# The 17-tap convolution of a graph network: one 136-point transform per graph in place of two 80-point windows

## The chip, the core and the metric

The kernel runs on one NeuronCore of a Trainium2 chip. The metric is device time in microseconds (us) of one execution. The kernel before has a median of 1908.61 us over 3 runs (1906.02 to 1911.41).

## The reference

A batch of 128 graphs with 128 nodes and 256 channels, all in float32, passes through two layers. The change concerns one convolution of the first layer, `conv2_w` with 17 taps along the node axis:

```python
h = relu(layernorm(x))                                  # (128, 128, 256)
xc = transpose(h, (0, 2, 1))
c = relu(bn1(conv1d(xc, conv1_w, pad=0)))               # 1 tap, 256 -> 256 channels
c = bn2(conv1d(c, conv2_w, pad=8))                      # 17 taps, 256 -> 256 channels
x_conv = transpose(relu(c + xc), (0, 2, 1))
s = h @ w_se.T + b_se;  A = exp(-dist(s, s)) * adj;  msg = relu(h @ w_msg.T + b_msg)
x_nmp = A @ msg
gi = concat([x_conv, x_nmp]) @ w_ih.T + b_ih;  gh = h @ w_hh.T + b_hh
r, z = sigmoid(gi_r + gh_r), sigmoid(gi_z + gh_z);  n = tanh(gi_n + r * gh_n)
x = x + (1 - z) * n + z * h
# second layer: five small graph convolutions on the first 25 nodes of each graph, added to x
```

## The kernel before, in words

The 17-tap convolution is done in the frequency domain. Each graph's 128 nodes are cut into two windows of 64 outputs; each window is transformed with `LW = 80` points (64 outputs and 16 neighbours), so there are `NP_ = 40` pairs of rows per window (real and imaginary part of a frequency). The work goes through these stages:

1. **Heads with the spectra of the weights** (`heads`, `some_spectra`). The graphs go in blocks of four (`BB = 4`). For each block: load x (`ln`, L184), layer norm on VectorE (L193 to L204), transpose on TensorE (L214), the 1-tap convolution (L228), a bias on VectorE (L231) and a ReLU on ScalarE (L232), then the forward transform (L243, `fd`, 160 columns: two windows of 80) and its copy into the big tile X in SBUF (L249 VectorE, L251 ScalarE). Between the blocks the taps are transformed: `weight_spectra` multiplies 17-row slices of the taps, four of them at partitions 0, 32, 64 and 96, with the 80 columns of `gt` (L167), and copies the results out of four PSUM banks (L173, L175). The spectra go to DRAM (`vd`, L177). Each step is 16 products; 32 steps are spread over the first 16 blocks.
2. **Frequencies of the first half** (`spectral`). X holds 64 graphs times two windows, 128 rows, so the whole batch needs two halves. For every frequency p the spectra of the weights are read from DRAM (`v`, L296, through SP's queue), GpSimd adds two of them (`vs`, L311), and six products of 128 rows by 256 columns follow (L314 two, L319 four; four products at p = 0, L304). VectorE adds (L320) into `ys`, which ScalarE's queue writes to DRAM (`yd`).
3. **Heads of the second half**, 16 blocks, with no taps left. Their first loads are issued in the course of stage 2 (`heads_begin`, called from `amid` at p = 16 and later); the weights of the gates are loaded here.
4. **Frequencies of the second half**, with GpSimd's sums for the gate weights (`gate_weights`) in between.
5. **Gates**, 32 blocks, some three quarters of the span: message passing (L535, L573, L585, L600), the inverse transform (`conv_out`), and the recurrent gates as Strassen-like products (L649), the second layer (L914, L974, L893) interleaved.

`conv_out` rebuilds the convolution of a block from `ym` (rows 0 to 127 of the 160 rows of each graph) and `yr` (the other 32 rows of each of the four graphs, together 128 rows). For each half o of the channels it takes one PSUM bank, four products with `idm` (L512, 128 columns each) and one with `idr` (L515, all 128 rows, 256 columns), then VectorE scales and adds (L517) and ScalarE applies the ReLU (L518). It is a generator: half 1 runs some steps after half 0, from `beside_gates`, which deals these pieces out between the products of the gates.

All PSUM tiles come from one pool of eight banks (`bank()`), handed out in a ring in the order in which the program asks: the ninth request gets the bank of the first, and its first product waits until that bank has been read out. TensorE takes its instructions in order.

SP's queue issues nearly all loads in an order written out by hand up to the end of stage 3 (`manual_schedule`); GpSimd's order is by hand up to the end of stage 4; the rest is placed by the scheduler.

Of the kernel before, what the change touches and what calls it, by code (L numbers as in the profile page):

```python
# [13 lines left out]
P = 128  # L14
# [4 lines left out]
HG = 64  # L19
OUTW = 64  # L20
LW = 80
NP_ = LW // 2
WCH = 64
NR = 2 * LW - P
# [51 lines left out]
def gnn_kernel(ctx: ExitStack, tc: tile.TileContext, io, out0: bass.AP, out1: bass.AP):  # L76
# [6 lines left out]

    NBH = HG // BB
    NH = B // HG

# [16 lines left out]
    fd = hc.tile([P, 2 * LW], F32)  # L103
# [46 lines left out]
    yd = [dram.tile([HG, 2, LW, D], F32, tag=f"yd{h}", name=f"yd{h}") for h in range(NH)]  # L150
# [9 lines left out]
    def weight_spectra(pool, c, q, w2):  # L160

        sp = pool.tile([P, LW, WCH], F32, tag="sp", name="sp", bufs=2)
        for t in range(WCH // 16):
            ps = [bank() for _ in range(4)]
            for j in range(4):
                for r in range(4):
                    nc.tensor.matmul(ps[r][:, j * LW:(j + 1) * LW], w2[32 * r:32 * r + KW, 4 * t + j, :],  # L167
                                     gt[32 * r:32 * r + KW, :], start=True, stop=True)
            for r in range(4):
                o0 = t * 16 + 4 * r  # L170
                dst, s = sp[:, :, o0:o0 + 4], ps[r][:, :4 * LW].rearrange("p (j d) -> p d j", j=4)
                if r == 3 and t < WCH // 16 - 1:
                    nc.vector.tensor_copy(dst, s)  # L173
                else:
                    nc.scalar.copy(dst, s)  # L175
            yield
        nc.scalar.dma_start(vd[c, q], sp)  # L177
# [57 lines left out]
    def head_spectra(X, i):  # L235
        h1 = h1s.pop(i)
        g0 = (i * BB) % HG
        for c in range(C):
            xv = X[:, c].rearrange("p a k (w g) -> p (a k) w g", w=2)
            for h in range(BB // 2):  # L240
                ps = bank()
                for bb in range(2):
                    nc.tensor.matmul(ps[:, bb * 2 * LW:(bb + 1) * 2 * LW], h1[:, 2 * h + bb, c * P:(c + 1) * P], fd,  # L243
                                     start=True, stop=True)
                s = ps[:, :4 * LW].rearrange("p (g w d) -> p d w g", g=2, w=2)
                dst = xv[:, :, :, g0 + 2 * h:g0 + 2 * h + 2]
                for w in range(2):
                    if h:
                        nc.vector.tensor_copy(dst[:, :, w], s[:, :, w])  # L249
                    else:  # L250
                        nc.scalar.copy(dst[:, :, w], s[:, :, w])  # L251

    def heads_begin(wk, xk, ahead, h):

        i = h * NBH
        for k in range(ahead):
            head_load(xk, ahead, i + k, nc.sync)
        yield
        for k in range(3):
            head_stats(wk, i + k)  # L260
            yield
            if k < 2:
                head_norm(i + k)
        head_turn(wk, i)

    def heads(wk, xk, ahead, X, h, between):

        i0, i1 = h * NBH, (h + 1) * NBH
        for i in range(i0, i1 + 1):
            if i + ahead < i1:  # L270
                head_load(xk, ahead, i + ahead, nc.sync)
            if i < i1:
                head_conv1(wk, i)
            between()
            if i + 1 < i1:
                head_turn(wk, i + 1)
            if i + 2 < i1:
                head_norm(i + 2)
            between()
            if i > i0:  # L280
                head_spectra(X, i - 1)
            if h == 0 and i % 2:
                between()
            if i + 3 < i1:
                head_stats(wk, i + 3, h1s[i] if h else None)

    def spectral(bp, X, h, amid):

        for p0 in range(0, NP_, 4):
            amid.get(p0, lambda: None)()  # L290
            ys = bp.tile([P, 4, 2, D], F32, tag="ys", name="ys", bufs=2)
            for p in range(p0, p0 + 4):
                if p % 2 == 0:
                    v = bp.tile([P, C, D // WCH, 4, WCH], F32, tag="v", name="v", bufs=3)
                    for c in range(C):
                        nc.sync.dma_start(v[:, c], vd[c, :, :, 2 * p:2 * p + 4, :].rearrange("q i d o -> i q d o"))  # L296
                vr, vi = v[:, :, :, 2 * (p % 2), :], v[:, :, :, 2 * (p % 2) + 1, :]
                a, d = X[:, :, p, 0, :], X[:, :, p, 1, :]
                y = ys[:, p - p0]
                ps = bank()  # L300
                if p == 0:
                    for k, (u, w) in enumerate(((a, vr), (d, vi))):
                        for c in range(C):
                            nc.tensor.matmul(ps[:, k * D:(k + 1) * D], u[:, c], w[:, c], start=c == 0, stop=c == C - 1)  # L304
                    nc.scalar.copy(y.rearrange("p k o -> p (k o)"), ps)
                    continue

                s = bp.tile([P, C, P], F32, tag="s", name="s", bufs=2)
                nc.vector.scalar_tensor_tensor(s, a, -2.0, d, op0=ALU.mult, op1=ALU.subtract)  # L309
                vs = bp.tile([P, C, D // WCH, WCH], F32, tag="vs", name="vs", bufs=3)  # L310
                nc.gpsimd.tensor_tensor(vs, vr, vi, op=ALU.add)  # L311
                p1 = bank()
                for c in range(C):
                    nc.tensor.matmul(p1[:, :D], a[:, c], vs[:, c], start=c == 0, stop=c == C - 1)  # L314
                k1 = bp.tile([P, D], F32, tag="k1", name="k1", bufs=2)
                nc.scalar.copy(k1, p1[:, :D])  # L316
                for k, (u, w) in enumerate(((s, vi), (d, vr))):
                    for c in range(C):
                        nc.tensor.matmul(ps[:, k * D:(k + 1) * D], u[:, c], w[:, c], start=c == 0, stop=c == C - 1)  # L319
                nc.vector.tensor_tensor(y, ps.rearrange("p (k o) -> p k o", k=2),  # L320
                                        k1[:, None, :].to_broadcast([P, 2, D]), op=ALU.add)
            for w in range(2):
                nc.scalar.dma_start(yd[h][:, w, 2 * p0:2 * p0 + 8, :].rearrange("g d o -> g (d o)"),
                                    ys[w * HG:(w + 1) * HG].rearrange("p a k o -> p (a k o)"))

# [27 lines left out]

    with front as es:
        hk = es.enter_context(tc.tile_pool(name="hk", bufs=1))
        xp = es.enter_context(tc.tile_pool(name="xp", bufs=1))
        X = xp.tile([P, C, NP_, 2, P], F32)
        order = es.enter_context(ExitStack())
        order.enter_context(tc.manual_schedule(engines={nc.gpsimd.engine}))
        sync_order = order.enter_context(ExitStack())  # L360
        sync_order.enter_context(tc.manual_schedule(engines={nc.sync.engine}))
        with ExitStack() as ws:
# [5 lines left out]
            ahead = 5  # L368
# [38 lines left out]
            heads(hk, xk, ahead, X, 0, some_spectra)  # L407
            while spectra or todo:
                some_spectra()
        gw = ctx.enter_context(tc.tile_pool(name="gw", bufs=1, side="right", reuse_waits="tile"))  # L410
        xk = es.enter_context(tc.tile_pool(name="xk1", bufs=1, reuse_waits="tile"))
        bp = es.enter_context(tc.tile_pool(name="bp", bufs=1, reuse_waits="tile"))
# [8 lines left out]
        def small_loads():  # L421
# [3 lines left out]

        begin = heads_begin(hk, xk, 3, 1)
        sums = gate_weights()
        amid = {p: lambda: next(begin, None) for p in range(16, NP_, 4) if p != 20}
        spectral(bp, X, 0, amid)
        for _ in begin:  # L430
            pass

        def gate_loads():
            yield
            small_loads()
            yield
# [3 lines left out]
            yield  # L440
            nc.sync.dma_start(wih[:, C:], io["wih"][D:].rearrange("(c p) o -> p c o", p=P))
            yield
            yield
            nc.sync.dma_start(whh, io["whh"].rearrange("(c p) o -> p c o", p=P))

        loads = gate_loads()
        heads(hk, xk, 3, X, 1, lambda: next(loads, None))
        sync_order.close()
        spectral(bp, X, 1, {p: lambda: next(sums, None) for p in range(4, NP_, 4)})
# [8 lines left out]
    loaded, hts = {}, {}  # L458

    def load(i):  # L460
        h, g0 = divmod(i * BB, HG)
        at = wk.tile([P, BB, N], F32, tag="at", name="at", bufs=2)
        yr = wk.tile([P, D], F32, tag="yr", name="yr", bufs=2)
        ym = wk.tile([P, BB, D], F32, tag="ym", name="ym", bufs=2)
# [3 lines left out]
        y = yd[h].rearrange("g w d o -> g (w d) o")[g0:g0 + BB]  # L468
        nc.sync.dma_start(ym, y[:, :P, :].rearrange("g r o -> r g o"))
        for b in range(BB):  # L470
            nc.sync.dma_start(yr[b * NR:(b + 1) * NR, :], y[b, P:, :])
        loaded[i] = at, ym, yr
        hts[i] = ht

    idr = wk.tile([P, BB, N - OUTW], F32)
    nc.sync.dma_start(idr, io["idr"])

    lr = wk.tile([P, 2, BB, 32], F32)
    nc.gpsimd.memset(lr, 0.0)
    nc.gpsimd.memset(lr[:, 0, :, 3:4], -1.0)  # L480
    nc.gpsimd.memset(lr[:, 1, :, 4:5], 1.0)

# [21 lines left out]
    def conv_out(i):  # L504

        ht = hts[i]
        _, ym, yr = loaded[i]
        xc = wk.tile([P, C, T], F32, tag="xc", name="xc", bufs=2)
        for o in range(C):
            ps = bank()  # L510
            for b in range(BB):
                nc.tensor.matmul(ps[:, b * N:(b + 1) * N], ym[:, b, o * P:(o + 1) * P], idm,  # L512
                                 start=b == 0, stop=False)

            nc.tensor.matmul(ps.rearrange("p (b n) -> p b n", b=BB)[:, :, OUTW:], yr[:, o * P:(o + 1) * P], idr,  # L515
                             start=False, stop=True)
# [61 lines left out]
    def edges(i):  # L578

        at, _, _ = loaded.pop(i)  # L580
# [629 lines left out]
```

## Time and profile before

| what | value |
|---|---|
| median of 3 runs | 1908.61 us |
| span of the profiled execution, first to last instruction | 1904.7 us |
| TensorE busy (PE) | 1881.7 us, 99% |
| VectorE busy (DVE) | 1345.3 us, 71% |
| ScalarE busy (ACT) | 723.9 us, 38% |
| GpSimd busy (POOL) | 667.7 us, 35% |
| mean granted TensorE clock | 0.996 |
| bytes moved by DMA | 265.87 MB |

The page gives no time of the profiled execution but its span; the median of the runs stands 3.9 us above it.

In the profile a float32 product appears as two MATMUL records (two passes), so counts of records are twice the counts in the code. A record's own duration contains the pipeline's latency; what a product costs TensorE is read from the distance between the starts of neighbouring groups in the timeline. The stages lie at about 0 to 161 us (heads and taps), to 274 us (first frequencies), to 376 us (second heads), to 479 us (second frequencies), and from there on the gates.

### The profile page before, as it was taken

The numbers are of one execution on the slowest core, as the hardware profiler recorded it, in microseconds if no ns is written. First come the engines' busy times: TensorE is split into PE (matmuls) and PEld (weight loads), VectorE is DVE, ScalarE is ACT, GpSimd is POOL, SyncE is SP. The second block draws the span as 40 slices with busy tenths as digits, with TensorE's granted clock in tenths as the row PEclk, the third lists the DMA queues.
The fourth block names the chain that finished last, engine by engine and source line by source line (L and its number), as shares of the span: only waits on it lengthen the run. The fifth ranks groups of instructions, "written<-read, shape, count | busy, mean of one in ns | idle before, by whom it ended". The sixth has DMA issues, their size and how long they took to land.

```text
span 1904.7 us, 31441 instructions
## 1 busy us (share of the span) xinstructions
PE 1881.7 (99%) x10994; PEld 1646.3 (86%) x10994; DVE 1345.3 (71%) x3246; ACT 723.9 (38%) x1588; POOL 667.7 (35%) x747
## 2 busy tenths in 40 slices
PE   9999999999999999999999999999999999999998
PEld 7889889988888888888888888888888888888887
DVE  6775558754778788887666777888666688787643
ACT  5552124411333433343343343343343434334334
POOL 1113431265335445444312244544322244444200
PEclk9999999999999999999999999999999999999999
DMA  9976995289732332233233433233234423222135
GB/s 349 328 295 221 306 321 206 100 286 315 235 89 73 97 87 73 73 98 97 73 106 96 131 89 85 73 88 108 81 89 101 137 74 108 65 78 72 36 92 152
DMA packets 248877, 265.87 MB, mean 140 GB/s; under 512 B 106866, under 2 KB 223943, under 8 KB 244239
## 3 DMA queue, kind: packets, MB, share of 16 engines
q1 hardware_dynamic: 238751, 199.82, 36.6%
q10 hardware_dynamic: 9968, 64.04, 8.6%
q8 instruction: 88, 1.44, 0.3%
q14 instruction: 70, 0.57, 0.1%
HBM read 178.66 MB, written 85.14 MB: 139 GB/s over the span
## 4 chain that ended last, share of the span: by engine, by line
PE 92%; DVE 3%; DMA 3%; POOL 1%; issue 1%; ACT 0%; SPq 0%; POOLq 0%; DVEq 0%; ACTq 0%
PE bank L649 45%; PE bank L319 6%; PE bank L974 5%; PE bank L535 5%; PE bank L914 5%; PE bank L228 4%; PE bank L314 3%; PE bank L600 3%; PE bank L243 3%; PE bank L512 3%; PE bank L167 2%; DMA v<-vd 1%; PE bank L515 1%; PE bank L893 1%; PE bank L214 1%; PE bank L825 1%
## 5 line engine op out<-in xcount | busy, mean ns | idle before, releaser
L649 PE MATMUL bank<-t,sw 128*128 128x256 f32 x1152 | 291.1, 380 | 0.0
L662 POOL TENSOR_TENSOR u<-u,m 128x256 f32<-128x256 f32 x128 | 94.8, 741 | 486.5 <-ACT m L660 442.4
L649 PEld LDWEIGHTS bank<-t,sw 128*128 128x128 f32 x1152 | 215.6, 190 | 29.6 <-issue 2.3
L649 PE MATMUL bank<-t,wih 128*128 128x256 f32 x768 | 197.2, 379 | 0.0
L649 PEld LDWEIGHTS bank<-t,wih 128*128 128x128 f32 x768 | 143.4, 190 | 19.3 <-issue 0.5
L311 POOL TENSOR_TENSOR vs<-v 128x512 f32<-128x512 f32 x78 | 101.4, 1320 | 113.5 <-DMA v<-vd 61.1
L228 PE MATMUL bank<-wc,ht 128*128 128x256 f32 x512 | 119.9, 387 | 1.4 <-ACT ht L215 1.4
L649 PE MATMUL bank<-t,whh 128*128 128x256 f32 x384 | 115.3, 382 | 2.8 <-DVE u L667 2.8
L649 PE MATMUL bank<-xc,wih 128*128 128x256 f32 x384 | 117.0, 386 | 0.7 <-DVE nh L664 0.2
L558 ACT ACTIVATE msg<-msg 128x512 f32<-128x512 f32 x64 | 36.8, 622 | 209.6 <-DVE msg L554 209.6
L974 PE MATMUL bank<-w,hh 128*125 128x256 f32 (+9 forms) x480 | 113.5, 380 | 1.5 <-DVE hh L919 1.5
L649 PE MATMUL bank<-xn,wih 128*128 128x256 f32 x384 | 114.2, 379 | 0.0
L228 PEld LDWEIGHTS bank<-wc,ht 128*128 128x128 f32 x512 | 97.0, 194 | 15.8 <-ACT ht L215 2.9
L649 PE MATMUL bank<-ht,whh 128*128 128x256 f32 x384 | 110.0, 380 | 0.0
L914 PE MATMUL bank<-ax,w 128*128 128x500 f32 (+8 forms) x416 | 106.9, 396 | 0.0
L198 POOL TENSOR_TENSOR rs<-ve,mhalf 128x4 f32<-128x4 f32 x32 | 32.8, 1026 | 205.5 <-DVE ve L196 205.5
L309 DVE SCALAR_TENSOR_TENSOR s<-X 128x256 f32<-128x256 f32 x78 | 49.9, 642 | 75.8 <-PE bank L319 75.2
L974 PEld LDWEIGHTS bank<-w,hh 128*125 128x125 f32 (+9 forms) x480 | 84.3, 177 | 19.8 <-DVE hh L919 1.9
L694 ACT ACTIVATE nn<-nn,vec 128x512 f32<-128x512 f32 x64 | 46.2, 722 | 135.0 <-DVE nn L693 135.0
L316 ACT COPY k<-bank 128x256 f32<-128x256 f32 x78 | 28.9, 373 | 171.8 <-DVE ys L320 79.7
L667 DVE TENSOR_TENSOR u<-bank,u 128x256 f32<-128x256 f32 x128 | 53.4, 417 | 57.7 <-PE bank L649 57.5
L649 PEld LDWEIGHTS bank<-xc,wih 128*128 128x128 f32 x384 | 70.5, 190 | 19.3 <-DVE nh L664 10.8
(207 smaller groups left out, 4537.6 us busy)
## 6 DMA issues: line engine op xcount, KB each, us to landing
v<-vd SPq DMA_DIRECT2D x80, 512.0 KB
vd<-sp ACTq DMA_DIRECT2D x8, 2560.0 KB
yd<-ys ACTq DMA_DIRECT2D x40, 512.0 KB
w<-in_w_dram SPq DMA_DIRECT2D x40, 512.0 KB
ln<-in_x_dram SPq DMA_DIRECT2D x32, 512.0 KB
htd<-ht ACTq DMA_DIRECT2D x32, 512.0 KB
ht<-htd SPq DMA_DIRECT2D x32, 512.0 KB
ym<-yd SPq DMA_DIRECT2D x32, 512.0 KB
```

The lines of the kernel that those rows point to most:

```text
L228: nc.tensor.matmul(pv[:, bb, :], ht[:, c, b * N:(b + 1) * N], wc1[:, c, :], start=c == 0, stop=c == C - 1)
L243: nc.tensor.matmul(ps[:, bb * 2 * LW:(bb + 1) * 2 * LW], h1[:, 2 * h + bb, c * P:(c + 1) * P], fd, start=True, stop=True)
L311: nc.gpsimd.tensor_tensor(vs, vr, vi, op=ALU.add)
L314: nc.tensor.matmul(p1[:, :D], a[:, c], vs[:, c], start=c == 0, stop=c == C - 1)
L319: nc.tensor.matmul(ps[:, k * D:(k + 1) * D], u[:, c], w[:, c], start=c == 0, stop=c == C - 1)
L512: nc.tensor.matmul(ps[:, b * N:(b + 1) * N], ym[:, b, o * P:(o + 1) * P], idm, start=b == 0, stop=False)
L535: nc.tensor.matmul(ps[:, b, :], d[:, b * N:(b + 1) * N], w, start=True, stop=True)
L600: nc.tensor.matmul(ps[:, b * N:(b + 1) * N], msg[:, b, c * P:(c + 1) * P], e[:, b, :], start=True, stop=True)
L649: nc.tensor.matmul(ps, w, d, start=n == 0, stop=n == len(pairs) - 1)
L662: nc.gpsimd.tensor_tensor(got["u4"], got["u2"], got["m5"], op=ALU.add)
L914: nc.tensor.matmul(pv[:, q - q0, :], w1s[k5 + g][:, c, q * P:(q + 1) * P], xv[:, c], start=c == 0, stop=c == C - 1)
L974: nc.tensor.matmul(ps[:n1, :D], hh[:, q, at:at + n1], w2s[k5 + g][:, q, :], start=q == 0, stop=q == HID // P - 1)
```

## The change

One transform of `LW = 136` points (128 outputs and 8 of padding, cyclically) covers a whole graph. X then holds 128 graphs in one go, so one phase of heads and one phase of frequencies remain:

- `NP_` is 68 in place of 40 frequencies, passed once in place of twice. `fd` has 136 columns in place of 160, `gt` 136 in place of 80.
- The taps are transformed in 64 steps of 8 products in place of 32 steps of 16, spread over all 32 blocks of heads.
- X is two tiles, X0 (the first `NB = 20` frequencies) and X1; X0 is given back after p = 19 and the gate weights are loaded into its place (`gate_loads` at p = 24 to 36).
- `v` comes in tiles of one channel half and four frequencies, five buffers; GpSimd's sum is two instructions of 256 elements per partition in place of one of 512.
- `yd` has 128 rows per graph, `yrd` the other `NR = 8` rows. For a block of four graphs `yr` now holds 2 halves x 4 graphs x 8 rows: 32 rows for each channel half, at partitions 0 and 32.
- `conv_out` takes both banks at once, first does the two products with `idr` (32 rows, 512 columns each), then the four products with `idm` of half 0, and after its `yield` the four of half 1.
- The order at the start of the gates: the first unit of gates of block 0 runs ahead of `conv_out(0)`.
- `dynamic_dma_scratch_size=256` is given where the program is set up.

```diff
-HG = 64
-OUTW = 64
-LW = 80
+LW = P + PAD
 NP_ = LW // 2
-WCH = 64
-NR = 2 * LW - P
+NB = 20
+WCH = 32
+NR = LW - P
...
     def weight_spectra(pool, c, q, w2):
-        for t in range(WCH // 16):
+        for t in range(WCH // 8):
             ps = [bank() for _ in range(4)]
-            for j in range(4):
+            for j in range(2):
                 for r in range(4):
-                    nc.tensor.matmul(ps[r][:, j * LW:(j + 1) * LW], w2[32 * r:32 * r + KW, 4 * t + j, :],
+                    nc.tensor.matmul(ps[r][:, j * LW:(j + 1) * LW], w2[32 * r:32 * r + KW, 2 * t + j, :],
                                      gt[32 * r:32 * r + KW, :], start=True, stop=True)
...
     def head_spectra(X, i):
-                    nc.tensor.matmul(ps[:, bb * 2 * LW:(bb + 1) * 2 * LW], h1[:, 2 * h + bb, c * P:(c + 1) * P], fd,
+                    nc.tensor.matmul(ps[:, bb * LW:(bb + 1) * LW], h1[:, 2 * h + bb, c * P:(c + 1) * P], fd,
                                      start=True, stop=True)
...
+            if p % 4 == 0:
+                amid.get(p, lambda: None)()
+                for c in range(C):
+                    v[c] = bp.tile([P, D // WCH, 8, WCH], F32, tag="v", name="v", bufs=5)
+                    nc.sync.dma_start(v[c], vd[c, :, :, 2 * p:2 * p + 8, :].rearrange("q i d o -> i q d o"))
...
-                nc.gpsimd.tensor_tensor(vs, vr, vi, op=ALU.add)
+            for c in range(C):
+                nc.gpsimd.tensor_tensor(vs[:, c], vr[c], vi[c], op=ALU.add)
...
-        begin = heads_begin(hk, xk, 3, 1)
-        sums = gate_weights()
-        amid = {p: lambda: next(begin, None) for p in range(16, NP_, 4) if p != 20}
-        spectral(bp, X, 0, amid)
-        for _ in begin:
-            pass
...
-        heads(hk, xk, 3, X, 1, lambda: next(loads, None))
-        sync_order.close()
-        spectral(bp, X, 1, {p: lambda: next(sums, None) for p in range(4, NP_, 4)})
+        loads, sums = gate_loads(), gate_weights()
+        amid = {p: lambda: next(loads, None) for p in range(24, 40, 4)}
+        amid.update({p: lambda: next(sums, None) for p in range(40, NP_, 4)})
+        spectral(bp, (X1, NB), NB, NP_, amid)
...
     def conv_out(i):
-        for o in range(C):
-            ps = bank()
+        pss = [bank() for _ in range(C)]
+        for o, ps in enumerate(pss):
+            g = slice(o * BB * NR, (o + 1) * BB * NR)
+            nc.tensor.matmul(ps, yr[g, :], idr[g, :], start=True, stop=False)
+        for o, ps in enumerate(pss):
             for b in range(BB):
                 nc.tensor.matmul(ps[:, b * N:(b + 1) * N], ym[:, b, o * P:(o + 1) * P], idm,
-                                 start=b == 0, stop=False)
-
-            nc.tensor.matmul(ps.rearrange("p (b n) -> p b n", b=BB)[:, :, OUTW:], yr[:, o * P:(o + 1) * P], idr,
-                             start=False, stop=True)
+                                 start=False, stop=b == BB - 1)
             nc.vector.scalar_tensor_tensor(xc[:, o, :], ps, sc2[:, o:o + 1], ht[:, o, :], op0=ALU.mult, op1=ALU.add)
             nc.scalar.activation(xc[:, o, :], xc[:, o, :], AF.Relu, bias=sh2[:, o:o + 1])
             yield
...
-    held = [6]
+    held = [7]
     def sums_ahead():
         held[0] -= 1
         if held[0] == 0:
+            for _ in conv_out(0):
+                pass
+            gate_inputs(0, (0,))
             for _ in begin:
                 pass
             gate_inputs(0, (1,))
...
-    nc = bacc.Bacc("TRN2", target_bir_lowering=False, num_devices=1)
+    nc = bacc.Bacc("TRN2", target_bir_lowering=False, num_devices=1, dynamic_dma_scratch_size=256)
```

## The prediction

> **What bounds the kernel now.** I read the page first: busy time, the chain that ended last, the costliest groups.
>
> ```profile
> PE 1881.7 (99%) x10994; PEld 1646.3 (86%) x10994; DVE 1345.3 (71%) x3246; ACT 723.9 (38%) x1588; POOL 667.7 (35%) x747
> ```
> ```profile
> PE 92%; DVE 3%; DMA 3%; POOL 1%; issue 1%; ACT 0%; SPq 0%; POOLq 0%; DVEq 0%; ACTq 0%
> ```
>
> TensorE is the bound from end to end, so each microsecond of products added or removed counts, and so does each gap. What a product costs I read from the timeline of TensorE: the distance between starts, not the record's duration.
>
> ```profile
> 144.64 2.34 PE L243 MATMUL bank<-fd,h 128*128 128x160 f32 x16
> 146.82 3.62 PE L228 MATMUL bank<-wc,ht 128*128 128x256 f32 x16
> 150.27 1.04 PE L214 MATMUL bank<-ident,ln 128*128 128x128 f32 x8
> ...
> 167.23 1.03 PE L319 MATMUL bank<-v,X 128*128 128x256 f32 x4
> 168.10 1.03 PE L314 MATMUL bank<-vs,X 128*128 128x256 f32 x4
> ```
>
> Two records are one product. 16 records of 160 columns take 2.18 us, 16 of 256 take 3.45 us, 8 of 128 take 0.87 us (150.27 to the next group at 151.15), 4 of 256 take 0.865 us: about 0.85 ns per column and record, so 0.272 us for a product of 160 columns, 0.4325 us for 256. No floor shows down to 128 columns. Products of few rows at partitions 0, 32, 64, 96 are cheaper:
>
> ```profile
> 26.92 1.13 PE L167 MATMUL bank<-gt,w 17*128 17x80 f32 x32
> 27.99 3.72 PE L228 MATMUL bank<-wc,ht 128*128 128x256 f32 x16
> ```
> ```profile
> 512.23 0.59 PE L649 MATMUL bank<-xn,wih 128*128 128x256 f32 x2
> 512.75 0.50 PE L585 MATMUL bank<-lt 5*128 5x128 f32 x8
> 513.18 0.70 PE L649 MATMUL bank<-xc,wih 128*128 128x256 f32 x2
> ```
>
> 32 records of 80 columns take 1.07 us and 8 of 128 take 0.43 us: half of a full product's price, and proportional to the columns. The group ahead of and the one behind such a burst take 0.10 us each too long (0.52 and 0.54 in place of 0.43): entering and leaving costs 0.20 us; for the 32 bursts of L167 I find 0.19 us each.
>
> The gaps I read from the busy time by stretches of 5 us (columns: stretch, length, PE, PEld, DVE, ACT, POOL, granted clock, DMA share, GB/s):
>
> ```profile
> 200.00:205.00 5.00, 2.44 (x10) 1.85 (x10) 4.64 (x15) 0.75 (x2) 1.83 (x2) 0.95 1.08 382
> 205.00:210.00 5.00, 5.00 (x18) 4.13 (x17) 0.74 (x2) 0.40 (x2) 3.29 (x3) 0.71 1.10 363
> 275.00:280.00 5.00, 3.94 (x20) 3.21 (x19) 2.09 (x10) 1.69 (x4) 1.02 (x1) 1.00 1.05 400
> ```
>
> At 200 us the second half's x loads, on SP's queue among the `v` loads, starve GpSimd's `vs`, then the clock is cut. Starts against 0.85 ns per column give the loss: 5.2 us at 200 to 240, 2.5 us at 274 to 283 where the second heads start.
>
> **What the Trainium skill says.** "TensorEngine Tiling (Array Packing)", Key Properties: changing the tiling mode drains TensorE, and tiles run in parallel. The trace agrees on the drain (0.20 us per burst) but shows a factor of 2, not up to 4. "TensorE: Matmul & The Clock Gate", Part 3, The mechanism: matmuls start and end strictly in program order; so a product that waits for its bank holds up all behind it. The same page, Part 1: idle stretches of some 3 us cut the clock; the trace agrees (0.71 after the 2.56 us gap at 203 us).
>
> **The change part by part**, against the span of 1904.7 us.
>
> *Frequencies.* Before: 2 x (39 x 6 + 4) = 476 products of 256 columns; after: 67 x 6 + 4 = 406. 70 x 0.4325 = **-30.3 us**.
>
> *Forward transform, L243.* 256 products, 160 to 136 columns: 256 x 24 x 1.7 ns = **-10.4 us**.
>
> *Taps, L167.* 512 products, 80 to 136 columns at 0.84 ns (two records, half price): 0.067 to 0.114 us, **+24.3 us**. Both measured points (80, 128 columns) lie on one line. The 64 bursts in place of 32 pay 32 x 0.19 = **+6.0 us**.
>
> *`idr`, L515.* Before, two full products of 256 columns, 0.865 us per block, no change of mode. After, two products of 32 rows and 512 columns in two row groups. No row shows two groups. Half price, as with four: 0.865 us, and I take that; two groups cannot do better than halve, so no gain. If nothing overlaps: 1.73 us, +27.7 us in all. Mode change: 32 x 0.20 = **+6.5 us**.
>
> *Second heads go.* The losses at 200 to 240 and at 274 to 283 had their loads and their start as cause: **-7.7 us**. In their place come 2.8 MB of gate weights on SP's queue ahead of `v` loads at p = 24 to 36. One frequency needs 0.79 MB in 2.6 us (303 GB/s), the rate seen is some 340 (337 at a DMA share of 0.96, 175 to 200 us); the five buffers hold about 1.5 groups of four ahead. I take **+1 us**, between 0 and 4. The weights wait for the last reader of X0, but by then no buffer is free for the `v` queued behind them.
>
> *Beside TensorE:* copies, hidden by products. Per block of heads TensorE needs 3.45 + 0.87 + 1.84 + 2.3 steps x (0.92 + 0.19) = 8.7 us; VectorE 4 x 0.58 (statistics) + 1.54 (norm) + 1.34 (bias) + 1.1 (X) + 0.7 (taps) = 7.0 us, 80%. In the second heads of before it stood at 80% (19.98 of 25 us) with TensorE at 25.00. GpSimd's sum, split in two at about 0.74 (the 256-element row L662), is 1.5 us of 2.6. Cost 0; without cover, VectorE's lateness would come through, up to 5 us.
>
> *Start of the gates.* The inverse of block 0 no longer covers the message chain (the gap of 2.23 us before L573 grows by its 1.3 us), while the 1.4 us wait of L535 for GpSimd goes, since `ht` comes earlier: 0, within 4.
>
> *A new wait in the gates.* `conv_out` now takes both banks before half 0, and the second is filled only after its `yield`. In the instruction order of the changed kernel, built but not run, TensorE goes:
>
> ```
> L484 bank_10136 (idr), bank_10137 (idr)     L487 bank_10136 x4
> L621 bank_10152 x3, bank_10159 x3   L545 bank_10164   L785 bank_10169
> L621 bank_10183, bank_10187         L487 bank_10137 x4
> L621 bank_10196     L621 bank_10200 [waits DVE]
> ```
>
> The ring has eight banks. Counting requests, 10196 sits in 10136's bank and 10200 in **10137's**: it must wait until VectorE has read out 10137, which TensorE finished one product (0.43 us) earlier. In 26 of 32 blocks the listing has this distance; before, by the same count, no bank comes back within 1.2 us. What VectorE needs, the same place of before shows:
>
> ```profile
> 772.19 1.05 PE L512 MATMUL bank<-idm,ym 128*128 128x128 f32 x8
> ...
> 773.08 0.60 PE L515 MATMUL bank<-idr,yr 128*128 128x256 f32 x2
> ...
> 773.40 0.35 ACT L652 COPY m<-bank 128x256 f32<-128x256 f32 x1
> 773.51 0.59 PE L649 MATMUL bank<-t,sw 128*128 128x256 f32 x2
> 773.79 0.42 DVE L654 TENSOR_TENSOR nh<-bank,m 128x256 f32<-128x256 f32 x1 [0.19 <-ACT m L652]
> ...
> 773.95 0.59 PE L649 MATMUL bank<-t,whh 128*128 128x256 f32 x2
> 774.13 0.74 DVE L517 SCALAR_TENSOR_TENSOR xc<-bank,bn,ht 128x512 f32<-128x512 f32 x1
> ```
>
> L517 ends at 774.87, 2.7 us after the four `idm` products began at 772.19: it stands behind L654, which waits for L652, which waits behind a sigmoid for GpSimd. After, TensorE wants the bank 0.87 + 0.43 = 1.3 us after 772.19, at 773.49: short by 1.4 us. But half 0's group has grown by 0.63 us (0.43 + 0.20), which gives the chain that much lead: 0.8 us. From below, L517 starts 0.21 us after the products at best (seen in 4 blocks) and takes 0.74: 0.21 + 0.74 - 0.43, 0.55 us with the signal. Behind the waiting product stand all later gates. 26 x 0.8 = **+20.8 us**, between 14 and 36.
>
> *Sum:* -30.3 - 10.4 + 24.3 + 6.0 + 6.5 - 7.7 + 1 + 20.8 = **+10.2 us**. Span 1914.9; the median lies 3.9 us above the span, so 1908.6 + 10.2 = **1918.8 us**.
>
> **The rivals.**
>
> *The bank is free in time* (faster): the ring or the release works otherwise than I count, or VectorE gets ahead. The sum without it is -10.6: 1898 us. For it: products were saved, and TensorE hardly waits for VectorE now. Against: the listing shows a wait for VectorE on exactly that product. It decides from 0.4 us per block: 26 x 0.4 = 10.4 eats the gain.
>
> *The two `idr` products don't overlap, or by half.* Each block pays 0.43 to 0.87 us more (13.8 to 27.7 in all), while the bank's wait shrinks to its floor of 0.55 (26 x 0.55 = 14.3): -10.6 + 13.8 + 14.3 = +17.5 at half, +31.4 with none: 1926 to 1940 us.
>
> *The wait is at its floor* of 0.55 us, or the losses at the start of the gates shrink: -10.6 + 14.3 = +3.7, 1912 us, within 0.3%.
>
> *Starved frequencies or late VectorE:* +5 to +9 on the sum, 1924 to 1928 us.
>
> **How the numbers follow.** Forecast (0.8 us each) 0.40; wait at its floor 0.20; bank free 0.15; `idr` not overlapped 0.15; starved 0.10. A measurement of this kernel tells about 0.3%, 5.7 us, from no change: the limits are 1902.9 and 1914.3. Faster: the free bank, 0.15. Same: the floor, 0.20. Slower: the rest, 0.65. For 8 in 10 the range reaches into the free bank at the bottom (1899) and to `idr` without most of its overlap at the top (1936).
>
> **What would show it.** Right: frequencies at 2.6 us each over 68 of them; tap bursts of 0.92 us; between `idm` of half 1 and the second product after it about 0.8 us in which TensorE waits for VectorE's L489, in 26 blocks, some 20 us in TensorE's list of waits, where all of VectorE's entries together now hold less than 8. Wrong: no such wait, bursts of 0.5 us (a load floor rather than columns), `idr` pairs of 1.3 us or more, or `vs` waiting for `v` at p = 28 to 36.

## The result, and the profile after

The changed kernel takes 1900.66 us (median of 7 runs, 1897.6 to 1904.94), the kernel before 1910.94 us on the same chip. The ratio is 0.9949, with a 95% interval from 0.9932 to 0.9965: faster by 10.3 us. Measured again on another occasion the ratio was 0.9953 (0.9935 to 0.9972). The forecast was 1918.8 us, slower; what came is the first rival, "the bank is free in time", at 1898 us.

From the page of the changed kernel, busy time and the chain that ended last:

```profile
PE 1872.8 (98%) x10854; PEld 1606.5 (84%) x10854; DVE 1352.3 (71%) x3248; ACT 743.7 (39%) x1667; POOL 666.1 (35%) x803
```
```profile
PE 93%; DVE 3%; DMA 2%; POOL 0%; issue 0%; ACT 0%; ACTq 0%; SPq 0%; DVEq 0%; POOLq 0%
```

The picture is that of before. What the forecast staked everything on is in TensorE's list of waits (who waited for whom: us in total, times, longest):

```profile
PE bank L545 <- DVE lr L538: 4.2, 1, 4.2
PE bank L621 <- DVE xc L489: 3.5, 1, 3.5
...
PE bank L302 <- POOL vs L299: 3.1, 1, 3.1
PE bank L165 <- ACT sp L173: 2.3, 1, 2.3
```

L621 should have stood there some 26 times for VectorE's L489. It stands there once, at 539 us, where the gates start up. The place in a settled block, from the timeline:

```profile
764.09 1.05 PE L487 MATMUL bank<-idm,ym 128*128 128x128 f32 x8
...
764.47 0.35 ACT L624 COPY m<-bank 128x256 f32<-128x256 f32 x1
764.86 0.42 DVE L626 TENSOR_TENSOR nh<-bank,m 128x256 f32<-128x256 f32 x1 [0.19 <-ACT m L624]
...
764.98 0.60 PE L621 MATMUL bank<-t,sw 128*128 128x256 f32 x2
765.20 0.74 DVE L489 SCALAR_TENSOR_TENSOR xc<-bank,bn,ht 128x512 f32<-128x512 f32 x1
...
765.41 0.59 PE L621 MATMUL bank<-t,whh 128*128 128x256 f32 x2
```

The product that was to wait for L489 starts at 765.41, 0.43 us after the one ahead. L489 starts only at 765.20 and ends at 765.94, so it is still reading, and the product cannot be in its bank. VectorE is late as forecast, by 0.53 us rather than 0.8: the forecast's floor was 0.55. The built program says which bank each PSUM tile has (tile, bank), and I had counted instead of reading it:

```
bank_10136 1   bank_10137 5   bank_10152 7   bank_10159 0   bank_10164 3   bank_10169 4
bank_10183 2   bank_10187 6   bank_10196 1   bank_10200 7   bank_10206 0   ...   bank_10224 5
```

Up to 10196 this looks like a ring. Then 10200 gets bank 7, whose tile 10152 had long been read, and 10137's bank 5 comes back only with 10224. It is no ring: 5 is next in turn and still in use, and the tile gets another bank that is free. The sentence on the ring in the section on the kernel before is wrong in the same way.

**The stages,** from the first starts of their products on TensorE in the profiled executions (1904.7 us before, 1902.1 us after; they differ by 2.6 us only, so that of before is a quick one and that of after a long one, and its second profile has 1899.3):

| stage | before | after | difference | forecast |
|---|---|---|---|---|
| heads and taps, both halves | 262.8 | 283.3 | +20.5 | +17.4 (-10.4 + 24.3 + 6.0 - 2.5) |
| frequencies, both halves | 212.4 | 180.4 | -32.0 | -34.5 (-30.3 - 5.2 + 1) |
| gates to the end | 1425.5 | 1434.9 | +9.4 | +27.3 (6.5 + 20.8) |

### The profile page after: what moved, and what is told of

Its sections match the earlier page's. It is cut to its first block, busy times and chain, and to the rows that moved or that the text cites. A ratio compares the mean times of both kernels' runs of the same rounds, so it can differ in the third digit from the quotient of the medians.

```text
span 1902.1 us, 31103 instructions
## 1 busy us (share of the span) xinstructions
PE 1872.8 (98%) x10854; PEld 1606.5 (84%) x10854; DVE 1352.3 (71%) x3248; ACT 743.7 (39%) x1667; POOL 666.1 (35%) x803
## 4 chain that ended last, share of the span: by engine, by line
PE 93%; DVE 3%; DMA 2%; POOL 0%; issue 0%; ACT 0%; ACTq 0%; SPq 0%; DVEq 0%; POOLq 0%
PE bank L621 46%; PE bank L307 6%; PE bank L947 5%; PE bank L507 5%; PE bank L887 5%; PE bank L226 5%; PE bank L240 3%; PE bank L487 3%; PE bank L572 3%; PE bank L302 3%; PE bank L165 2%; PE bank L484 2%; PE bank L212 2%; PE bank L866 1%; PE bank L798 1%; PE bank L557 1%
## 5 line engine op out<-in xcount | busy, mean ns | idle before, releaser
L621 PE MATMUL bank<-t,sw 128*128 128x256 f32 x1152 | 291.9, 380 | 3.5 <-DVE xc L489 3.5
L621 PEld LDWEIGHTS bank<-t,sw 128*128 128x128 f32 x1152 | 211.3, 191 | 30.4 <-DVE xc L489 3.7
L621 PE MATMUL bank<-t,wih 128*128 128x256 f32 x768 | 197.2, 379 | 0.0
L621 PEld LDWEIGHTS bank<-t,wih 128*128 128x128 f32 x768 | 143.4, 190 | 19.3 <-DVE u L639 0.5
L299 POOL TENSOR_TENSOR vs<-v 128x256 f32<-128x256 f32 x134 | 99.0, 762 | 73.2 <-PE bank L302 38.9
L621 PE MATMUL bank<-t,whh 128*128 128x256 f32 x384 | 115.1, 381 | 0.0
L621 PE MATMUL bank<-xc,wih 128*128 128x256 f32 x384 | 114.8, 381 | 0.0
L621 PE MATMUL bank<-xn,wih 128*128 128x256 f32 x384 | 114.5, 380 | 0.0
L621 PE MATMUL bank<-ht,whh 128*128 128x256 f32 x384 | 111.0, 383 | 0.0
L639 DVE TENSOR_TENSOR u<-bank,u 128x256 f32<-128x256 f32 x128 | 53.6, 418 | 57.2 <-PE bank L621 57.0
L296 DVE SCALAR_TENSOR_TENSOR s<-X 128x256 f32<-128x256 f32 x67 | 45.1, 675 | 68.8 <-PE bank L307 68.8
L887 PEld LDWEIGHTS bank<-ax,w 128*128 128x128 f32 x416 | 70.2, 191 | 20.4 <-issue 12.3
L487 PEld LDWEIGHTS bank<-idm,ym 128*128 128x128 f32 x512 | 64.4, 191 | 25.9 <-issue 23.5
```

What stands on the lines that cost most here:

```text
L299: nc.gpsimd.tensor_tensor(vs[:, c], vr[c], vi[c], op=ALU.add)
L621: nc.tensor.matmul(ps, w, d, start=n == 0, stop=n == len(pairs) - 1)
L887: nc.tensor.matmul(pv[:, q - q0, :], w1s[k5 + g][:, c, q * P:(q + 1) * P], xv[:, c], start=c == 0, stop=c == C - 1)
```

## The experiments

Times are medians; where two kernels did not share a chip, each is compared through its ratio to the kernel before. A "burst" is a run of short products that have few rows and lie side by side at several partitions, as L557 once in each block. "Block" is the time from one burst of L557 to the next in settled blocks of the gates: 36.94 us in the changed kernel (its bursts stand at 655.12, 692.06 and 729.00 us), 36.84 us before. Six later distances are longer: in the changed kernel 63.0, 66.77 and 49.33 us, twice each; the last two kinds are called the four long blocks.

**The forecast's case made by hand.** Two kernels. Both have seven banks in the common pool and one beside it, and TensorE's order of the gates written out as it was. In *seven_one* only half 1 of `conv_out` uses the eighth; in *shared_bank* the product j = 5 uses it as well, the one that was to wait.

```diff
-        pss = [bank() for _ in range(C)]
+        pss = [bank(), bank("cv")]
...
-                ps = bank()[:, :H]
+                ps = bank("cv" if j == 5 and pairs == (2,) else "bank")[:, :H]   # shared_bank alone
```

> The changed kernel with seven banks in the common pool and the eighth held for half 1 of conv_out alone (TensorE's order of the gates written out as it was); no product comes to a bank sooner than 1.1 us after TensorE filled it. Theory (what the forecast missed is only which bank the product gets): nothing waits, the time is the changed kernel's 1901 us within 4. Rival (one bank less in circulation already costs): L621 waits for VectorE or ScalarE at the 52 places where a bank comes back after 1.1 us, at 0.1 to 0.3 us each, 1906 to 1916 us.

> As seven_one, but the fourth product of the gates' candidate unit (j = 5) takes the bank of conv_out's half 1, so that in 26 blocks TensorE wants this bank 0.43 us after the idm products that filled it: the forecast's case made by hand. Theory (the forecast's chain was priced rightly, only the bank was not the one): L621 waits for VectorE's L489 in 26 blocks for some 0.6 us (L489 ended 0.96 us after the last idm product at 764 us, and the product between takes 0.43), 10 to 20 us over seven_one, and the list of TensorE's waits shows it. The forecast itself: 0.8 us in each, 21 us. Rival (VectorE gets ahead once TensorE waits, or the release works otherwise): below 4 us over seven_one, no such entry.

*seven_one* took 1916.8 us (ratio 1.0037, 1.0024 to 1.005), *shared_bank* 1926.7 us (1.0088, 1.0073 to 1.0104). TensorE's waits of *shared_bank* and its timeline at the same place:

```profile
PE bank L621 <- DVE xc L489: 14.9, 27, 2.6
```
```profile
771.75 0.60 PE L621 MATMUL bank<-t,sw 128*128 128x256 f32 x2
771.95 0.75 DVE L489 SCALAR_TENSOR_TENSOR xc<-bank,bn,ht 128x512 f32<-128x512 f32 x1
...
772.75 0.70 PE L621 MATMUL bank<-t,whh 128*128 128x256 f32 x2 [0.41 <-DVE xc L489]
```

Now the wait is there, in 26 blocks (the list has 27: one wait at the start of the gates is in the changed kernel too), and the product starts 1.00 us after the one ahead where 0.43 would do. So the mechanism was sound, and only the bank was not the one. The price was not: by the starts the product is late by 0.57 us in 25 blocks (more in the first) rather than by 0.8, and of that only 0.38 us reaches the block (37.32 to 37.70 us). The starts show where the other 0.2 us went. In *seven_one* TensorE stands 0.2 us in 25 blocks ahead of a later product, the one behind L798, for VectorE's `nh`; in *shared_bank*, where that product comes later anyway, this wait is gone. The time is 9.9 us longer rather than 20.8.

In *seven_one* the rival was right, at the upper end of its range: one bank less in circulation costs some 17 us against the changed kernel by the ratios (12 to 15 us between the profiled executions), with 0.38 us in each settled block of the gates and 5 us in the heads (288.4 us).

**The same wait, longer.** *shared_next*: the product j = 6, straight after the `idm` products, gets the bank.

> As shared_bank, but the third product of the unit (j = 6), which comes straight after the idm products of half 1, takes their bank: distance 0 rather than 0.43 us, in 30 blocks. Theory (the wait is as long as the readout needs, and part of it comes back as lead for the waits after it, as in shared_bank where 0.67 us in 26 blocks, 17.4 us, made 9.9 us of time): 1.1 us in each, 28 to 33 us of waits, and 16 to 21 us over seven_one's 1916.8 us, 1933 to 1938 us. Rival (a wait costs its full length): 28 to 33 us over seven_one, 1945 to 1950 us.

1940.3 us (1.0174, 1.0155 to 1.0192), some 26 us over *seven_one* by the ratios. The block is 38.12 us.

```profile
PE bank L621 <- DVE xc L489: 29.9, 30, 5.5
```

The cost lies between the two expectations: waits of 1.0 us by the starts in 29 blocks, and a longer one at the start of the gates; 0.8 us of them is in the block. What comes back is again 0.2 us, the same wait behind L798, which is gone here too. So a wait costs its full length less the later waits that it covers; it is not a share of the wait that comes back.

**Do the two `idr` products run side by side?** *unpaired*: each half takes its bank when it comes to it and does its own `idr` product ahead of its `idm` products.

```diff
-        pss = [bank() for _ in range(C)]
-        for o, ps in enumerate(pss):
+        for o in range(C):
+            ps = bank()
             nc.tensor.matmul(ps, yr[g, :], idr[g, :], start=True, stop=False)
-        for o, ps in enumerate(pss):
```

> The changed kernel with each half of conv_out taking its own bank when it comes to it and doing its idr product alone, right ahead of its idm products. Theory (half price comes from two row groups side by side): each of the two products costs 0.87 us rather than 0.43, and there are two changes of mode at some 0.4 us rather than one: 0.87 + 0.4 = 1.3 us per block, less what it saves in waits, 27 to 41 us more than the changed kernel. Rival (32 rows alone are at half price): one more change of mode at 0.2 to 0.4 us, 6 to 13 us more.

1935.5 us (1.0138, 1.0111 to 1.0164), 36 us more than the changed kernel: the theory. The pair in the changed kernel (four records), and one product alone (two records) in *unpaired*:

```profile
684.26 1.13 PE L484 MATMUL bank<-idr,yr 32*128 32x512 f32 x4
...
685.32 1.16 PE L487 MATMUL bank<-idm,ym 128*128 128x128 f32 x8
...
686.31 1.46 PE L621 MATMUL bank<-t,sw 128*128 128x256 f32 x6
```
```profile
757.18 0.59 PE L620 MATMUL bank<-xn,sw 128*128 128x256 f32 x2
757.71 1.12 PE L484 MATMUL bank<-idr,yr 32*128 32x512 f32 x2
758.76 1.16 PE L486 MATMUL bank<-idm,ym 128*128 128x128 f32 x8
```

The pair holds TensorE for 1.06 us, the single one for 1.05. A product of 32 rows alone is no cheaper than a full one (0.87 us at 0.85 ns per column and record, the rest is the change of mode); the second, at other partitions, is free.

**What does the pair cost the kernel?** *no_idr* leaves it out.

```diff
-            nc.tensor.matmul(ps, yr[g, :], idr[g, :], start=True, stop=False)
...
-                                 start=False, stop=b == BB - 1)
+                                 start=b == 0, stop=b == BB - 1)
```

> The changed kernel without its idr products: the last 8 of the 136 rows of the inverse transform are left out. Theory: the pair costs TensorE 1.28 us in each of 32 blocks (0.87 itself, 0.42 for the two changes of mode), 41 us, of which 7 to 9 come back, since VectorE's chain loses the lead and TensorE waits for nh again as before the change (0.28 us per block): 33 us less than the changed kernel, 1867 to 1870 us. Rival (nothing waits): 41 us less, 1860 us. Rival (the forecast's price, 0.87 with 0.20 for the modes, and waits): 26 us less, 1875 us.

1887.9 us (0.9886, 0.987 to 0.9901): 12 us less, where the smallest of the three expectations was 26. My theory of the price failed. From the starts, 0.09 + 1.06 + 0.12 us are gone from each block, and the settled block fell from 36.94 to 36.84 us only. The four long blocks did fall by the full 1.26 us (66.77 to 65.51 and 49.33 to 48.07). Together this is some 7 us; most of the rest lies where nothing was changed, in the heads, which last 280.1 us here and 283.3 in the changed kernel (the losses below). In the settled blocks TensorE waits for VectorE instead:

```profile
PE bank L618 <- DVE nh L633: 10.6, 25, 0.4
```

The starts show 0.58 us of delay at this product and smaller ones behind the bursts and transposes next to it. 36.84 us is also the block of the kernel before, which led to the next run.

**Is TensorE the bound in the gates at all?** *before_no_idr* is the kernel before without its L515.

> The kernel before without its idr products: the last 32 of the 160 rows of the inverse transform are left out, 0.865 us of TensorE's products in each of the 32 blocks, 27.7 us. In no_idr a block of the gates still takes 36.83 us from one edges burst to the next, after as many us were taken from TensorE as it had gained; the kernel before has 36.83 us too. Theory (at this point of a block the chain of VectorE, ScalarE and GpSimd is as long as TensorE's products, so that what TensorE saves comes back as waits for nh): the block stays within 0.25 us of 36.83, TensorE waits for nh some 0.9 to 1.1 us per block, and the time falls by 0 to 8 us. Rival (TensorE alone sets the block in the kernel before): 36.0 us per block, 27 us less, 1881 us.

1905.2 us, a ratio of 0.9983 (0.9972 to 0.9993): 27.7 us of products taken away, some 3 us gained. The settled block is 36.84 us, as before: nothing of what was taken out shows there. The four long blocks are shorter by 0.87 us each (66.38 to 65.51 and 48.94 to 48.07), all that was taken out of them, and that is the gain (4 x 0.87 = 3.5 us). Its page and its waits:

```profile
PE 1863.0 (98%) x10866; PEld 1622.6 (85%) x10866; DVE 1347.2 (71%) x3246; ACT 724.4 (38%) x1588; POOL 667.0 (35%) x747
```
```profile
PE bank L646 <- DVE nh L661: 10.6, 25, 0.4
```

The theory holds for the settled blocks; in the long ones TensorE is the bound. The chain that ended last, followed through a block of *no_idr*, leaves TensorE there for 6.3 us (start, us, what):

```profile
681.58 0.23 PE bank L542 x2
681.82 0.74 DVE xc L486
682.56 0.34 DVE u L636
682.97 0.74 POOL o L637
683.73 0.72 ACT o L654
...
687.68 0.44 DVE nh L633
688.16 1.99 PE bank L618 x8
```

In this stretch VectorE, GpSimd and ScalarE take turns, and their chain is longer than TensorE's products in it, some 5 us by their prices. In *before_no_idr* the chain lies on VectorE nearly without a break from 648.8 to 659.8 us just ahead of such a stretch, so an earlier end of the `idm` products does not start it earlier: what TensorE saves at the inverse it stands waiting a few products later. In *no_idr* the chain is on TensorE just ahead of the stretch; why the stretch does not start earlier there is not shown. "PE 98%" tells nothing of all this. The Trainium skill warns of this in "Perfetto Trace Analysis", Identifying the Most-Contended Engine: matmul busy time is no good measure of how close a kernel is to its limit. The run agrees: busy time fell by 18.7 us, the time by 3.

**The two losses in heads and frequencies.** In the changed kernel TensorE lost 2.3 us at 150 us and 3.1 us at 358 us, with a stretch of lower granted clock behind each (0.60 over 154 to 159 us, 0.82 over 360 to 365 us). For the first, the timeline has the issue of a taps load on ScalarE's queue just ahead of its copies:

```profile
149.97 2.73 ACTq L153 DMA_DIRECT2D w<-in_w2t_dram  x1
...
152.74 0.98 ACT L173 COPY sp<-bank 128x272 f32<-128x272 f32 x3 [2.56 <-issue]
...
153.18 0.73 PE L165 MATMUL bank<-gt,w 17*128 17x136 f32 x10 [2.26 <-ACT sp L173]
```

*taps_sp* issues these loads from SP; *late_loads* puts the gate weights later; *both_loads* does both; *later_loads* does both, with all gate weights behind the release of X0.

```diff
-                            taps.append(taps_load(wp, *todo[2], nc.scalar))   # taps_sp
+                            taps.append(taps_load(wp, *todo[2], nc.sync))
...
-        order.enter_context(tc.manual_schedule(engines={nc.gpsimd.engine}))
+        order.enter_context(tc.manual_schedule(engines={nc.gpsimd.engine, nc.sync.engine}))
...
-        amid = {p: lambda: next(loads, None) for p in range(24, 40, 4)}
-        amid.update({p: lambda: next(sums, None) for p in range(40, NP_, 4)})
+        amid = {p: lambda: next(sums, None) for p in range(40, NP_, 4)}
+        for p in (24, 28, 40, 52):        # late_loads; later_loads: (28, 32, 40, 48); whh last in both
+            amid[p] = lambda s=amid.get(p): (next(loads, None), s and s())
```

> The changed kernel with the loads of the later taps issued from SP's queue rather than ScalarE's. Theory (the loss at 146 to 164 us comes from an issue of 2.7 us on ScalarE's queue that holds up its copies of sp): L165 no longer waits 2.3 us for L173 there, 2 to 6 us less than the changed kernel, 1895 to 1899 us. Rival (the transfer itself was late, whatever queue issues it, or SP's loads of x now come later in its place): within 1 us, or up to 3 us more.

> The changed kernel with its gate weights loaded later and further apart: the small ones at p = 24, the halves of wih at p = 28 and 40, whh at p = 52, SP's order written out up to the end of the frequencies. Theory (the loss at 355 to 370 us, a wait of 3 us of L302 for GpSimd's vs and then a lower clock, is caused by gate weights ahead of v in the queue): the stall goes, 3 to 5 us less than the changed kernel, 1896 to 1898 us. Rival (the queue is at its limit through the whole stage anyway and the stall only moves to p = 40 or 52): within 1 us of 1900.7 us.

> late_loads and taps_sp together, the version that should beat both kernels. Theory: the two losses lie in different stages and add, 5 to 10 us less than the changed kernel, 1891 to 1896 us. Rival: neither was the bound, within 2 us of 1900.7 us.

> taps_sp with the gate weights at p = 28 (the small ones), 32, 40 (wih) and 48 (whh), in an SP order written out by hand. In late_loads the small loads stood in the queue at p = 24, waited for the last reader of X0, and the transfers stood at 0 GB/s for some 1.5 us; here X0 is free by the time they are issued. Theory (the stall of L302 at 341 or 358 us comes from loads ahead of v, first by their wait and then by their bytes): no wait of L302 over 1 us, 3 to 5 us less than taps_sp's 1893 us, 1888 to 1891 us. Rival (the bytes as such, 2.8 MB on a queue near its limit, cost the stall wherever they are put): a wait of some 3 us later on, 1892 to 1896 us.

> The changed kernel once more, beside later_loads on the same chip: 1900.7 us within 3. If the 2.3 us wait of L165 for L173 at 150 us is an accident of a single execution, this profile may lack it and taps_sp's gain is smaller than 7 us; if it belongs to the kernel, it is there again.

| kernel | us | ratio to before |
|---|---|---|
| taps_sp | 1893.3 | 0.9927 (0.9911 to 0.9943) |
| late_loads | 1899.8 | 0.9961 (0.9945 to 0.9978) |
| both_loads | 1896.1 | 0.9944 (0.9926 to 0.9962) |
| later_loads | 1891.1 | 0.991 (0.989 to 0.9929) |
| after_again | 1899.6 | 0.9953 (0.9935 to 0.9972) |

*taps_sp* gains some 4 to 5 us by the ratios, though the intervals touch: each issue takes 0.34 to 0.46 us on SP, L165's wait for L173 is gone, the heads last 277.1 us in place of 283.3. Of the eight profiles with these loads on ScalarE's queue six have the wait (*after_again* 1.8 us), while *unpaired* and *late_loads* have none. Their heads last 277.6 and 278.1 us, and the products for which the changed kernel needs the 18.1 us from 146 to 164 us take 12.8 us in both. So the wait and the lower clock behind it cost 5.3 us there (4.5 us in *after_again*), and without them *taps_sp* gains 0.5 to 1 us in the heads. Why that one issue is long in six profiles and not in two is not shown. Of the 11 us between the two profiled executions 3 lie in the gates, where *taps_sp* changes nothing. *late_loads* gains nothing: the wait of L302 is 3.3 us, only earlier. Its order by hand put the small loads at p = 24 ahead of the `v` loads, and there they waited for X0's last reader:

```profile
332.87 0.35 SPq L415 DMA_DIRECT2D idm<-in_idm_dram  x1
```
```profile
330.00:334.00 4.00, 4.00 (x20) 3.51 (x20) 2.26 (x3) 0.37 (x1) 2.17 (x4) 1.00 0.15 61
334.00:338.00 4.00, 4.00 (x20) 3.54 (x19) 1.99 (x3) 0.74 (x2) 1.15 (x2) 1.00 0.94 257
```

The last two columns of the second view are the DMA share and GB/s: the transfers stood nearly still for 4 us. *both_loads* inherits this and misses its expectation: it is slower than *taps_sp* alone. In *later_loads* L302 is not among TensorE's waits any more, and the frequencies last 175.4 us rather than 180.4 or 178.7. It is the version that beats both kernels, 8.5 us under the changed kernel on the same chip, at the weak end of what was expected of it. Its gain over *taps_sp*, some 2 to 3 us, lies within the intervals.

## Why the prediction was wrong, step by step

**The failed step is "A new wait in the gates", +20.8 us.** The wait does not exist in the changed kernel: the sum without this step is -10.6 us, and -10.3 was measured. It failed twice.

- Its premise: "The ring has eight banks. Counting requests, ... 10200 in 10137's." The bank assignment is no ring. The wait that the listing showed on that product, for VectorE, was taken as evidence for this bank; it belonged to something long done (L639's read of 10152, whose bank 10200 gets). The trace of after has the product starting while L489 still reads.
- Its price. Where the clash is made by hand, it costs 9.9 us: a settled block has 0.57 us rather than 0.8 (close to my floor of 0.55), and 0.2 us of it replaces another wait, which comes from the bank that *seven_one* lacks. With the price of that run my sum would have stood at -10.6 + 9.9 = -0.7 us. With eight banks that other wait is absent, and up to 25 x 0.57 = 14 us might be lost, +4 us (an estimate; no run shows it). Either is no change by the limits of the prediction, even if the bank had been the one I counted.

That the remaining sum fits to 0.3 us is luck in part: two of its steps, on the taps and on the engines beside TensorE, are wrong by some 15 and 10 us and largely cancel. The other steps, against the stages:

- *"TensorE is the bound from end to end"*: wrong for the settled blocks of the gates, where taking out 0.87 us of products gained nothing (*before_no_idr*).
- *Frequencies, -30.3,* and *L243, -10.4*: the counts of records and the prices hold. Together they are what the change saves.
- *Taps, +24.3*: too high by some 15 us. Bursts of the changed kernel, one that is held up (38.08) and one that is not (40.62):

```profile
38.08 0.64 PE L165 MATMUL bank<-gt,w 17*128 17x136 f32 x4
38.93 0.73 PE L165 MATMUL bank<-gt,w 17*128 17x136 f32 x12 [0.22 <-DVE h L229]
39.60 1.09 PE L212 MATMUL bank<-ident,ln 128*128 128x128 f32 x8
40.62 0.75 PE L165 MATMUL bank<-gt,w 17*128 17x136 f32 x16
41.30 2.12 PE L240 MATMUL bank<-fd,h 128*128 128x136 f32 x16
43.26 2.97 PE L226 MATMUL bank<-wc,ht 128*128 128x256 f32 x13
```

  From 40.62 to 41.30 a burst takes 0.68 us, where I had 0.92. It takes that in 28 of the 61 bursts behind the first three. My "factor of 2" and the price per column were a misreading. In the single records of such a burst four, one at each group of 32 partitions, start within 0.02 us of each other, and the next four follow 0.12 us later, the time of a single record of 136 columns: a factor of 4, with 0.1 us more at each end of the burst. Before, with 80 columns, the next four follow after 0.11 us. So the wider transform costs next to nothing per round of four; 64 bursts of 0.68 us in place of 32 of 1.06 are +9.6 us.
- *Mode changes of the taps, +6.0*: right as priced, 0.15 to 0.20 us ahead of and behind a burst.
- *Beside TensorE, 0*: too low by some 10 us, and this hid the error of the taps. The bursts of *taps_sp* add up to some 15 us over 0.68 each, those of before to 5 us over 1.06 each: in the others the four records do not start together, or stand as at 38.93. The releasers that the trace names are mostly VectorE's L229 and ScalarE's L173; most of these waits are too short for the list. How they divide between the engines is not shown.
- *The load on ScalarE's queue* is in no step of mine. It accounts for 5.3 us of the profiled execution, and with it the heads came out 3 us above the forecast. The change keeps these loads going up to 220 us.
- *Second heads go, -7.7*: no run isolates it. Without the two new losses (heads of *taps_sp*, frequencies of *later_loads*) the two stages stand at +14.3 and -37.0 us against my +17.4 and -34.5, so nothing speaks against it; since the first agrees through two errors that cancel, little speaks for it either.
- *Gate loads, +1 (0 to 4)*: too low. *later_loads* has the frequencies 3 to 5 us shorter.
- *`idr`*: two row groups overlap in full, as assumed. The change of mode costs 0.41 us per block (0.09 ahead, 0.19 within, 0.12 behind), not 0.20. The four long blocks grew by 0.39 us, the settled ones by 0.10 us only, since the kernel before had some 0.28 us of waits for VectorE in them, which the longer `idr` group covers. I had not seen these: they show in the starts, and the list of waits has one of them alone.
- *Start of the gates, 0 within 4*: the wait of L545 for `lr` is 4.2 us where L573 had 2.2, and L535's 1.4 us are gone. Of the 9.4 us by which the gates grew, about 5 lie between the second and the last burst of L557, 1.3 at the start and 2.6 at the end. At the end the clock was cut (0.57 over 1882 to 1886 us); from the last burst on, the changed kernel takes 150.0 us, *taps_sp* 146.9 and *later_loads* 147.5, before 147.4. So these 2.6 us do not belong to the change.

The other rivals: no overlap of the `idr` products is refuted by *unpaired*; starved frequencies were real, at 3 to 5 us; late engines in the heads were real too, as the waits inside the bursts.

## What to carry to other kernels

A wait that is inferred from a bank or a buffer must rest on the program's own assignment, not on a count of requests; and a wait for an engine that is named in a listing is no proof that the engine is late. Before a product is priced as time, take one out and see which parts of its stage get shorter: here the gates gave back some 3 us for 27.7, all of it in four blocks of 32. Before a burst is priced by its columns, look at the distance between the starts inside it. Put loads neither on the queue of an engine whose copies are waited for, nor ahead of others while their own target is still being read.

## What the runs showed of the hardware

- A product of 32 rows and 512 columns holds TensorE for 1.05 us alone and 1.06 us together with a second one at the next 32 partitions. The Trainium skill, "TensorEngine Tiling (Array Packing)", Key Properties, says that tiles work in parallel and that a change of mode drains; both agree, the drain at 0.41 us around and within such a pair. With four groups of 32 partitions the factor is 4, and the change of mode is about the same: a burst of taps takes 0.68 us and 0.19 around it, of which four rounds of 0.116 us are work.
- An issue on ScalarE's queue took 2.73 us at 149.97 us and 0.45 us at 167.93 us, for loads of the same size (512 KB); the copy behind the long one stood for 2.56 us. From SP such a load took 0.34 to 0.46 us to issue.
- After the 2.26 us wait at 151 us, the clock that was granted in the 5 us from 154 us was 0.60 (the column behind the five engines):

```profile
154.00:159.00 5.00, 5.00 (x35) 4.32 (x36) 2.25 (x8) 3.34 (x12) 0.00 (x0) 0.60 0.92 257
```

  From 146 to 164 us TensorE lost 5.3 us against the executions without the wait, more than twice the gap. The prediction gave "some 3 us" for such a gap; here the clock was cut after 2.26 us, and around a wait of 1.8 us in *after_again* (0.57 over 152 to 156 us), while *no_idr* had the wait at 1.7 us and kept the full clock.
- One PSUM bank of eight taken out of circulation costs this kernel some 17 us, more than the whole change gains.
